# A convolution and a whitening on one core: pieces of the last pass hold one image, and the conv tiles x and y get two buffers each

## The chip, the cores and the metric

The kernel runs on one core of a Trainium2 chip. The metric is the time of one execution on the device in microseconds; the time before is a median of 928.11 us over 3 runs. The core has a matrix engine (PE, whose weight loads are listed apart as PEld), a vector engine (DVE), a scalar engine (ACT), GpSimd (POOL), and SP, which here does nothing but issue DMAs. Each engine works through its own list of instructions in order. All DMAs share the core's 16 DMA engines.

## The reference

Input x has 4 images of 64 channels of 256 x 256 pixels in float32. Two layers are computed:

- A convolution for each channel. Its kernel is the outer product of two filters of 256 taps, hx along one axis and hy along the other, that a small network with sines computes. So a channel's image is multiplied by one Toeplitz matrix on one side and by another on the other side: `y = conv(x, hx outer hy) + x * bias[channel]`.
- A whitening over the channels: with `x1` the result as a matrix of 64 rows (channels) and 262,144 columns (pixels of all images), `x1_s` every ninth column, `mean` its mean, `cov = x1_s @ x1_s.T / count + 0.01 I`, the output is `cov^(-1/2) @ (x1 - mean)`, with the inverse square root from five Newton-Schulz steps.

The whitening needs the covariance of all images before the first output can be computed, so the result of the convolution goes to memory (134 MB of traffic with the read back) and is read again in a last pass.

## The kernel before

**Stages.** First the filter network (to about 21 us of the span). Then the convolution (to 628 us). Then what is left of the covariance and the small matrix chain for the inverse square root (to 672 us). Then the last pass: pieces of y are read, multiplied by the whitening matrix, and written out (to 928 us).

**The convolution.** The work is cut in 32 steps `(g, n)`: eight channels (group g of 8) of image n. For g 0 to 5 the steps run over n within g; at the end they run over n, with g = 6 and 7 for each, so the last two groups of image 0 are done at steps 24 and 25, of image 1 at 26 and 27, and so on. A step is four channel pairs c = 0, 2, 4, 6, and one call of `group(first, second)` is made for each pair. It multiplies the pair `first` (its x tile) by the first Toeplitz matrix, and, interleaved on PE, the pair `second`, which had its first product two calls ago, by the second one (line 208). Then ACT copies the first product out of PSUM (line 338), and DVE computes `y = x * bias + product` for the second pair (line 343, two instructions). Up to three sampling copies on DVE follow (`pack`, line 252): they pick every ninth pixel of a finished y tile for the covariance, nine copies for each tile.

**The order on SP.** The lists of all engines are in program order (`tc.manual_schedule`). After the instructions of a group SP gets, in this order:

1. the store of the second pair to `y_d` (line 353), which waits for DVE's two y writes;
2. one load of a quarter of an x tile, two channels, 512 KB (line 103);
3. in some groups a part of a later filter matrix (line 178, 256 or 192 KB, 56 of them in all);
4. in some of the last groups one or two loads of pieces for the last pass (line 290, 2 MB each), as the table `early` says.

SP stands still while its next instruction waits for something. Which x quarter is loaded after which group is set by these lines:

```
part = (c - 2) // 2 % 4
to = i + 2 if c else i + 1
```

So the first quarter of step i+2 is sent after pair c = 2 of step i, the second after c = 4, the third after c = 6, and the fourth after c = 0 of step i+1: each is sent six groups before the group that first needs it. Tiles x ("in") and y ("out") come from one pool, `big`, with three buffers for each tag, 16 KB per partition a buffer.

**The last pass.** y is kept in two tensors `y_d[v]` of 128 rows, the 64 channels of image 2v and those of 2v+1. A piece `(v, q)` is 128 rows by 4096 pixels; there are 16 for each v. The pieces take over buffers of the convolution: `homes` lists 13 of them, `tssioitsoitos`, with t a filter matrix, s a sample tile, i an x tile, o a y tile; piece i goes to home i modulo 13. Eight pieces are sent before the convolution ends (`early`), five directly after, the others when a home has been written out. Each piece is multiplied by the whitening matrix for the upper and the lower 64 rows (line 521), shifted by ACT (line 526) and DVE (line 529), and written by a DMA that POOL issues (line 534). `covariance(n - 1)` (line 266) runs on PE before pair c = 4 of steps 27, 29 and 31.

## Time and profile before

| what | us |
|---|---|
| median of 3 runs (lowest, highest) | 928.11 (927.27, 928.23) |
| the profiled execution, its own time | 930.36 |
| its span | 928.2 |
| PE busy with matmuls in the span | 788.6 |
| DVE busy | 653.6 |
| ACT busy | 480.9 |
| filter stage / convolution / matrix chain / last pass, ends at | 21 / 628 / 672 / 928 |
| DMA, moved in the span | 285.56 MB, mean 308 GB/s |

The profile is of one execution. An engine's busy time counts its instructions, not its waits, and matmuls overlap, so a busy PE is not PE at its peak. A line "A <- B" among the waits says that A stood idle until B was done. For a DMA the time "to landing" runs from its issue on SP or POOL until its completion is signalled, so it holds the time that it stands behind other transfers. In the stretches, the last three numbers are the granted clock of PE (1.00 is full), the mean busy share of the DMA engines, and GB/s.

### The profile page before, as it was taken

Reading aid. Unit: us, or ns where it says so; the run is one execution under the profiler, and the core shown is the slowest. Engines: PE = TensorE matmul, PEld = TensorE weight load, DVE = VectorE, ACT = ScalarE, POOL = GpSimd, SP = SyncE. Lnnn points to the kernel's source line nnn. Section 1 sums busy time; section 2 is a strip of 40 time slices with the busy share of each in tenths; the row PEclk is TensorE's granted clock in tenths of the full one; section 3 lists DMA queues with packets and bytes.
Section 4 is the critical chain, followed back from the end, with each engine's and each line's share of the span. In section 5 each row is a group of like instructions: output and inputs, shape, how many; then the busy total and the mean of one; then the engine's idle time right before and its main releaser. Section 6 shows DMA issues by size and latency. Waiting matters only on the chain.

```text
span 928.2 us, 27807 instructions
## 1 busy us (share of the span) xinstructions
PE 788.6 (85%) x11814; PEld 631.0 (68%) x11814; DVE 653.6 (70%) x869; ACT 480.9 (52%) x791; POOL 31.8 (3%) x71
## 2 busy tenths in 40 slices
PE   3999999999999999999999999999787777765400
PEld 2899999999999999999999999998311111111100
DVE  3058687768777877787677866667599999996500
ACT  2345454545454544554554544441399888876500
POOL 3000000000000000000000000000010000000010
PEclk9999999999999999999999999999799999998755
DMA  4698888888888888879997769989999999999998
GB/s 145 189 275 257 251 258 261 248 258 258 252 251 262 260 248 261 262 237 280 284 277 236 234 189 332 326 288 392 417 407 429 430 428 429 431 430 431 431 430 340
DMA packets 115406, 285.56 MB, mean 308 GB/s; under 512 B 6831, under 2 KB 89172, under 8 KB 107604
## 3 DMA queue, kind: packets, MB, share of 16 engines
q1 hardware_dynamic: 108080, 216.08, 70.2%
q0 software_dynamic: 6336, 67.11, 17.0%
q8 instruction: 93, 1.52, 0.7%
q10 hardware_dynamic: 868, 0.60, 0.2%
q14 instruction: 29, 0.24, 0.1%
HBM read 149.35 MB, written 134.42 MB: 306 GB/s over the span
## 4 chain that ended last, share of the span: by engine, by line
PE 69%; issue 15%; DVE 9%; ACT 3%; DMA 2%; POOL 0%; POOLq 0%; ACTq 0%; DVEq 0%; SPq 0%
PE p L208 65%; DVE yi L529 8%; ACT yi L526 3%; DMA yi<-y_d 2%; PE pc L266 2%; PE pk L234 1%; POOL out_dram L534 0%; PE po L521 0%; DMA toep<-g_d 0%; DVE y L343 0%; PE ZY L436 0%; PE YT L436 0%; DVE scratch L154 0%; DVE samp L252 0%; PE pm L147 0%
## 5 line engine op out<-in xcount | busy, mean ns | idle before, releaser
L208 PE MATMUL p<-toep,x 64*64 64x64 f32 (+3 forms) x5120 | 595.6, 288 | 5.2 <-DMA toep<-g_d 4.7
L208 PE MATMUL p<-toep,o 64*64 64x64 f32 (+3 forms) x5120 | 589.2, 285 | 0.2
L208 PEld LDWEIGHTS p<-toep,x 64*128 64x128 f32 (+1 forms) x5120 | 548.3, 168 | 31.5 <-issue 5.6
L208 PEld LDWEIGHTS p<-toep,o 64*128 64x128 f32 (+1 forms) x5120 | 543.5, 166 | 11.8 <-POOLq L224 0.6
L338 ACT COPY o<-p 64x512 f32<-64x512 f32 x512 | 297.0, 580 | 317.9 <-PE p L208 310.1
L343 DVE SCALAR_TENSOR_TENSOR y<-x,bias,p 128x512 f32<-128x512 f32 x256 | 179.9, 743 | 162.7 <-PE p L208 162.2
L252 DVE COPY_PREDICATED samp<-mask,y 128x448 f32<-128x448 int32 (+3 forms) x288 | 281.0, 976 | 6.6
L529 DVE TENSOR_SCALAR yi<-po,shift 64x512 f32<-64x512 f32 x256 | 192.1, 750 | 23.4 <-PE po L521 16.7
L521 PE MATMUL po<-yi,W 64*64 64x512 f32 x1024 | 150.0, 653 | 63.1 <-DVE yi L529 40.9
L526 ACT ACTIVATE yi<-po,shift 64x512 f32<-64x512 f32 x256 | 174.9, 683 | 42.4 <-PE po L521 34.9
L521 PEld LDWEIGHTS po<-yi,W 64*64 64x64 f32 x1024 | 35.4, 141 | 176.9 <-DVE yi L529 127.8
L534 POOL DMA_DIRECT2D out_dram<-yi x44 | 23.7, 539 | 262.6 <-DVE yi L529 119.3
L420 POOL MEMSET chain<- 64x64 f32 x1 | 0.1, 146 | 616.6 <-PE p L208 616.6
L266 PEld LDWEIGHTS pc<-samp 128*64 128x64 f32 x464 | 14.4, 137 | 2.2 <-issue 1.4
L266 PE MATMUL pc<-samp 128*64 128x65 f32 x464 | 15.1, 223 | 0.7 <-ACT samp L243 0.4
L147 PE MATMUL pm<-scratch 128*128 128x128 f32 (+1 forms) x12 | 3.7, 466 | 8.8 <-ACT scratch L156 6.2
L274 DVE SCALAR_TENSOR_TENSOR cov<-pc,cov 128x65 f32<-128x65 f32 x4 | 0.9, 226 | 12.7 <-PE pc L266 12.7
L147 PEld LDWEIGHTS pm<-scratch 128*128 128x128 f32 (+1 forms) x12 | 2.9, 313 | 9.4 <-ACT scratch L156 6.8
L234 PE MATMUL pk<-y,pick 128*128 128x112 f32 (+1 forms) x36 | 7.7, 390 | 1.3 <-DVE y L343 1.3
L234 PEld LDWEIGHTS pk<-y,pick 128*128 128x128 f32 x36 | 7.3, 259 | 1.7 <-issue 1.7
L243 ACT COPY samp<-pk 128x116 f32<-128x116 f32 x1 | 0.3, 271 | 15.9 <-PE pk L234 15.9
L131 POOL TENSOR_SCALAR pick<-ident,rows 128x128 f32<-128x128 f32 x9 | 5.7, 649 | 0.0
(71 smaller groups left out, 41.8 us busy)
## 6 DMA issues: line engine op xcount, KB each, us to landing
x<-in_x_dram SPq DMA_DIRECT2D x128, 512.0 KB, 5.8
y_d<-y SPq DMA_DIRECT2D x128, 512.0 KB, 4.1
yi<-y_d SPq DMA_DIRECT2D x32, 2048.0 KB, 16.0
out_dram<-yi POOLq DMA_DIRECT2D x28, 2048.0 KB, 43.4
out_dram<-yi POOLq DMA_DIRECT2D x16, 512.0 KB, 8.4
toep<-g_d SPq DMA_DIRECT2D x28, 256.0 KB, 6.3
toep<-g_d SPq DMA_DIRECT2D x28, 192.0 KB, 5.7
toep<-g_d SPq DMA_DIRECT2D x2, 384.0 KB, 8.3
```

Source lines behind the costliest of these rows:

```text
L131: nc.gpsimd.tensor_scalar(pick[:, s, :], ident, rows[:, s : s + 1], None, ALU.mult)
L147: nc.tensor.matmul(pm, lhsT=wt, rhs=hs[u], start=True, stop=True)
L208: mm = nc.tensor.matmul(ps[q : q + w, m, HP * k : L], lhsT=src[parts, k // 2, m * P + q : m * P + q + w], rhs=t[parts, : stop : -1] if k e ...
L234: nc.tensor.matmul(pk[:, b, :, 0:nj], lhsT=pick[:, (s - b) % STEP, :], rhs=yt[:, cs, b, s : s + STEP * (nj - 1) + 1 : STEP], start=(s == 0 ...
L252: nc.vector.copy_predicated(dst, m, src)
L266: nc.tensor.matmul(pc[half], lhsT=samp[n][:, b, j, 0:C], rhs=samp[n][:, b, j, :], start=(b == 0 and j < 2), stop=(b == H2 - 1 and j >= NJ ...
L338: nc.scalar.copy(o1[to], units[u][0][0][fr])
L343: nc.vector.scalar_tensor_tensor(yt[:, c + u], xt[:, c + u], bias[:, ch : ch + 1], units[u][1][0], ALU.mult, ALU.add,)
L521: nc.tensor.matmul(po[u][halves[k]], lhsT=W[halves[u]], rhs=yt[halves[u], cols[k]], start=True, stop=True,)
L526: nc.scalar.activation(yt[halves[0], cols[k]], po[0][halves[k]], AF.Identity, bias=shift[halves[k]])
L529: nc.vector.tensor_scalar(yt[halves[1], cols[k]], po[1][halves[k]], shift[halves[k]], None, ALU.add)
L534: nc.gpsimd.dma_start(out=o[:, end - part : end], in_=yt[:, end - part : end])
```

## The change

It has these parts:

- `y_d` becomes four tensors, one for each image: 128 rows of 32,768 pixels, the upper half of the image's rows for 64 channels, then the lower half. A piece `(n, q)` holds one image; there are 8 for each n. The output tensor has the same layout, `(n, half, channel, pixel)`, and is put in the usual order on the host after the run.
- The store of a pair is issued as two DMAs, one for each half, 256 KB each.
- The pool `big` has two buffers for each tag in place of three; a new pool `epool` has two buffers of the same size, which only pieces use ("e"). The list of homes is `eetssitsoiots`, 13 as before.
- The x quarters: the first of step i+1 is sent after pair c = 4 of step i, the second after c = 6, the third after c = 0 of step i+1, the fourth after c = 2.
- The table `early` has other places: eight loads as before, the first after pair c = 4 of step 26 (before: step 28).

```diff
-    big = ctx.enter_context(tc.tile_pool(name="big", bufs=3))
+    big = ctx.enter_context(tc.tile_pool(name="big", bufs=2))
+    epool = ctx.enter_context(tc.tile_pool(name="epool", bufs=2))
...
-    y_d = [dram.tile([2 * C, PIX], F32, tag=f"y{v}", name=f"y_d{v}") for v in range(NB // 2)]
+    y_d = [dram.tile([H2 * C, PIX // H2], F32, tag=f"y{n}", name=f"y_d{n}") for n in range(NB)]
...
-    pieces = [(v, q) for v in range(NB // 2) for q in range(PIX // FP)]
+    pieces = [(n, q) for n in range(NB) for q in range(PIX // H2 // FP)]
...
-        {"t": (tpool, "toep"), "s": (spool, "samp"), "i": (big, "in"), "o": (big, "out")}[k]
-        for k in "tssioitsoitos"
+        {"t": (tpool, "toep"), "s": (spool, "samp"), "i": (big, "in"), "o": (big, "out"), "e": (epool, "extra")}[k]
+        for k in "eetssitsoiots"
...
-        nc.sync.dma_start(out=t, in_=y_d[v][:, q * FP : (q + 1) * FP])
+        nc.sync.dma_start(out=t, in_=y_d[n][:, q * FP : (q + 1) * FP])
...
-    early = {(28, 4): 1, (28, 6): 1, (29, 6): 1, (30, 4): 1, (31, 2): 1, (31, 4): 1, (31, 6): 2}
+    early = {(26, 4): 1, (26, 6): 1, (27, 4): 1, (28, 2): 1, (29, 6): 1, (31, 4): 2, (31, 6): 1}
...
-            row = n % 2 * C + g * CG + c
-            nc.sync.dma_start(
-                out=y_d[n // 2][row : row + 2, :].rearrange(
-                    "c (b p w) -> p (c b) w", p=P, w=L
-                ),
-                in_=yt[:, c : c + 2].rearrange("p c b w -> p (c b) w"),
-            )
+            for b in range(H2):
+                row = b * C + g * CG + c
+                nc.sync.dma_start(
+                    out=y_d[n][row : row + 2, :].rearrange("c (p w) -> p c w", w=L),
+                    in_=yt[:, c : c + 2, b],
+                )
...
-            xt = loaded_x.pop((g, n))
+            xt = loaded_x[g, n]
...
-                part = (c - 2) // 2 % 4
-                to = i + 2 if c else i + 1
-                if to < len(steps) and to > 1:
+                part = (c - 4) // 2 % 4
+                to = i + 1 if c >= 4 else i
+                if 1 < to < len(steps):
...
-        o = out[2 * v : 2 * v + 2].rearrange("u c h w -> (u c) (h w)")[:, q * FP : (q + 1) * FP]
+        o = out[n].rearrange("b c f -> (b c) f")[:, q * FP : (q + 1) * FP]
...
-    out = nc.dram_tensor("out_0_dram", (NB, C, L, L), F32, kind="ExternalOutput").ap()
+    out = nc.dram_tensor("out_0_dram", (NB, H2, C, PIX // H2), F32, kind="ExternalOutput").ap()
...
-    return r.results[0]["out_0_dram"]
+
+    y = np.asarray(r.results[0]["out_0_dram"]).reshape(NB, H2, C, PIX // H2)
+    return np.ascontiguousarray(y.transpose(0, 2, 1, 3)).reshape(NB, C, L, L)
```

More of the change, by code (lines that the diff above doesn't have):

```diff
@@ L274, in covariance @@
         nc.vector.scalar_tensor_tensor(cov, pc, 1.0 / NSAMP, cov, ALU.mult, ALU.add)
-    pieces = [(v, q) for v in range(NB // 2) for q in range(PIX // FP)]
+    pieces = [(n, q) for n in range(NB) for q in range(PIX // H2 // FP)]
     homes = [
-        {"t": (tpool, "toep"), "s": (spool, "samp"), "i": (big, "in"), "o": (big, "out")}[k]
-        for k in "tssioitsoitos"
+        {"t": (tpool, "toep"), "s": (spool, "samp"), "i": (big, "in"), "o": (big, "out"), "e": (epool, "extra")}[k]
+        for k in "eetssitsoiots"
     ]
     def load_y(i):
-        v, q = pieces[i]
+        n, q = pieces[i]
         pool, tag = homes[i % len(homes)]
-        t = pool.tile([P, FP], F32, tag=tag, name=f"yi_{v}_{q}")
-        nc.sync.dma_start(out=t, in_=y_d[v][:, q * FP : (q + 1) * FP])
+        t = pool.tile([P, FP], F32, tag=tag, name=f"yi_{n}_{q}")
+        nc.sync.dma_start(out=t, in_=y_d[n][:, q * FP : (q + 1) * FP])
         return t
@@ L506, in conv_whiten_kernel @@
     halves = [slice(u * C, (u + 1) * C) for u in range(2)]
-    for i, (v, q) in enumerate(pieces):
+    for i, (n, q) in enumerate(pieces):
         yt = loaded.pop(i)
-        o = out[2 * v : 2 * v + 2].rearrange("u c h w -> (u c) (h w)")[:, q * FP : (q + 1) * FP]
+        o = out[n].rearrange("b c f -> (b c) f")[:, q * FP : (q + 1) * FP]
         part = FP if 1 < i < len(pieces) - 2 else FP // 4
@@ L515, in conv_whiten_kernel @@
             po = [
-                psA.tile([P, 512], F32, tag="psA", name=f"po_{v}_{q}_{w}_{u}") for u in range(2)
+                psA.tile([P, 512], F32, tag="psA", name=f"po_{n}_{q}_{w}_{u}") for u in range(2)
             ]
```

## The prediction

> **What bounds the kernel now.** I read the stages first (busy time of each engine in stretches of the span, with granted clock, share of the DMA engines and GB/s):

> ```profile
> 60.00:628.40 568.40, 567.65 (x10063) 533.64 (x10062) 427.87 (x519) 281.47 (x486) 0.00 (x0) 1.00 0.85 262
> 628.40:672.00 43.60, 34.83 (x325) 25.31 (x323) 26.02 (x58) 10.22 (x21) 1.95 (x4) 0.80 1.01 410
> 672.00:928.20 256.20, 141.89 (x968) 32.84 (x967) 186.34 (x249) 169.28 (x248) 21.91 (x41) 0.87 0.99 419
> ```

> The first pair after the length is PE, the second its weight loads. Up to 628.4 PE has no gap (567.65 of 568.40 us): the convolution is bound by matmuls. From 628.4 on the DMA engines are full (1.01 and 0.99): the tail of 300 us is bound by bytes. So a change is worth something in the first stage only through PE, and in the tail only through bytes that were moved before 628.4.

> Next, whether PE ever waited for an x tile. Of all waits of line 208's matmuls on a DMA there is one, on a filter matrix at the start:

> ```profile
> PE p L208 <- DMA toep<-g_d: 4.7, 1, 4.7
> ```

> Then the pace of a group, from the timelines of SP and of DVE (start, length, instruction):

> ```profile
> 309.86 0.38 SPq L353 DMA_DIRECT2D y_d<-y  x1
> 310.28 0.50 SPq L103 DMA_DIRECT2D x<-in_x_dram  x1
> 310.82 1.48 SPq L178 DMA_DIRECT2D toep<-g_d  x1
> 314.08 0.38 SPq L353 DMA_DIRECT2D y_d<-y  x1
> 314.55 0.45 SPq L103 DMA_DIRECT2D x<-in_x_dram  x1
> ```
> ```profile
> 308.42 1.40 DVE L343 SCALAR_TENSOR_TENSOR y<-x,bias,p 128x512 f32<-128x512 f32 x2 [0.50 <-PE p L208]
> 309.75 2.99 DVE L252 COPY_PREDICATED samp<-mask,y 128x448 f32<-128x448 int32 x3
> 312.65 1.40 DVE L343 SCALAR_TENSOR_TENSOR y<-x,bias,p 128x512 f32<-128x512 f32 x2
> 317.56 1.41 DVE L343 SCALAR_TENSOR_TENSOR y<-x,bias,p 128x512 f32<-128x512 f32 x2 [3.52 <-PE p L208]
> ```

> Two groups take 317.56 - 308.42 = 9.14 us, one g = 4.57 us. PE releases DVE at 308.42, when it is about to begin the next group; DVE writes y until 309.82; SP, which was standing in that wait, sends the store at 309.86, 1.44 us after the group's end, and only then the x load behind it in its order. How long the x load takes, from issue to landing, least, median and most: over the whole kernel, then between 323 and 333 us, where no filter load stands in between:

> ```profile
> x<-in_x_dram SPq DMA_DIRECT2D x128, 512.0 KB, 5.8
> y_d<-y SPq DMA_DIRECT2D x128, 512.0 KB, 4.1
> ```
> ```profile
> DMA to landing us min/median/max: 4.6/4.8/5.0
> ```

> Today this latency costs nothing, since an x load is sent six groups (27 us) before its use.

> **The change part by part.**

> *x in two buffers: the lead shrinks from six groups to one.* The load of channels c, c+1 is now sent after group k, and group k+2 needs it in its very first matmuls; only group k+1 lies between. Only SP's order counts, and there the load still stands behind the store of group k. So, from the end of group k: 1.44 us to the store; from the store's issue to the landing of x 0.42 + 4.8 = 5.22 us; about 0.3 us (estimate, one weight load of 0.17 us and one matmul of 0.29 us from their rows, partly overlapped) until matmuls flow again. That is D = 6.96 us, and the cover is g = 4.57 us. End(k+2) = End(k) + D + g, hence 11.53 us for two groups where 9.14 were: 5.77 a group, +1.20. Steps 2 to 31 have 120 such groups: **+144 us**. Queued behind the waiting matmul on PE is the whole group, the second-stage products of the previous group too; ACT's copies, DVE's two y writes and SP's next store wait for that, and behind the store the next x load: the delay feeds itself, so it does not dissolve. Bounds: x landing at its overall median of 5.8 gives D = 7.96, 6.27 a group, +203; the shortest chain (the 314.08 store, 1.1 us after its group's end by the cadence, x at its least 4.4 us, a restart of 0.1 us) gives D = 6.0, 5.3 a group, +86. I take the value near +144, because the slower pace drains the queues: the DMA share of 0.85 becomes 0.85 x 4.57 / 5.77 = 0.67, as in the quiet stretch.

> [...]

> *Each store in two halves.* 128 DMAs of 512 KB become 256 of 256 KB. SP spends 0.42 us more per group. This puts the x load 0.42 us later, but its data start only when the store's 512 KB are through, more than 0.42 us after either way, so I cost it at nothing; uncovered it is 0.42 / 2 x 120 = +25 us. The packets stay 1 KB.

> *y in two buffers.* Step i first writes y in its third group; y of step i-2 is stored for good three groups earlier (landing 4.1 us) and its nine sampling copies, three a group, end two groups earlier. Nothing, unless DVE falls two groups (9 us) behind: it has 1.40 + 2.99 = 4.4 us of work a group.

> *Piece loads at step 26 instead of 28.* Eight of 2 MB still precede the end of the convolution, five of them now ahead of x loads that have no slack. In the old kernel those between 560 and 632 us took

> ```profile
> DMA to landing us min/median/max: 9.4/11.3/16.1
> ```

> and y stores behind them up to 14.7. At 430 GB/s 2 MB occupy the engines for 4.9 us. After x has landed, some 7 us after its group's end, the piece runs to 12; the next group's store, sent at 5.8 + 1.4 = 7.2 us, would have begun its data near 8, and starts near 12: 3 to 4 us late, and so its x load. Five loads at 3.3: **+16 us** (0 if they fall into gaps, 25 if all their bytes count). The covariance of an image, 116 matmuls before steps 27 and 29, 3.7 us, now runs while PE would wait: **-4**.

> *The tail.* At the end of the convolution as many pieces are loaded as before (five landed, three on their way), 13 slots are filled before the first result leaves, and reads and writes keep runs of 16 KB. One piece is sent 4.3 us earlier: **-2**, at best one piece, -5. Whether the other addresses change the 430 GB/s I can't see; 1% of 256 us is 2.6 either way.

> The sum on the profiled execution's span of 928.2 us: 144 + 16 - 4 - 2 = +154, 1082 us. That execution took 930.36 us in all, the median of the runs is 928.11; the same difference on the median gives **1082 us**.

> *The clock.* [...] The rows (stretches as above, clock third from the end):

> ```profile
> 648.00:660.00 12.00, 6.49 (x90) 4.87 (x85) 4.05 (x22) 2.28 (x7) 0.00 (x0) 0.74 1.01 424
> 720.00:780.00 60.00, 42.98 (x312) 8.79 (x312) 58.17 (x79) 53.11 (x78) 5.35 (x10) 1.00 1.01 430
> ```

> PE busy for 54% had 0.74, busy for 72% in short pieces 1.00. After the change PE is busy for 4.57 / 5.77 = 79%, with gaps of 1.2 us, or 2.4 us every second group. [...] if gaps at the piece loads did halve it, their few groups would cost some +5 more; if it fell throughout, see below.

> **Rivals.**
> 1. *The queue stays congested:* landing keeps the 5.8 us of the crowded stretches, since the load starts sooner after its store, and filter loads (56 of 256 or 192 KB) follow it. For it: the median itself; against it: the smaller DMA share. +203 + 16 - 6 = +213, 1140 us.
> 2. *The load is faster than I think*[...], 1015 to 1025 us.
> 3. *The clock falls:* matmuls at 0.75 would make g 6.1 us, (6.96 + 6.1) / 2 = 6.5 a group, +235, some 1170 us; at half clock more. Against it the 72% row.
> 4. *The other side:* PE doesn't wait, and the tail gains its piece: 923 to 928 us. This needs x to land within 4.57 us of the end of group k. It decides from D = g: the load would have to be on its way about 2.4 us earlier, which it can't while it stands behind a store that waits for DVE (1.44 us alone leaves 3.1 us, under the least landing of 4.4). That the change doesn't do what it says is the same case: the buffers do shrink and the order is written by hand.

> **How the numbers follow.** Chances: my case 0.56 (1050 to 1115), rival 1 0.21, rival 2 0.13, rival 3 0.06, rival 4 0.04. The likeliest is 1082 us. For 8 in 10 the range takes in most of rivals 1 and 2: 1022 to 1150. A difference under 0.2% can't be told from none here; faster 0.025, same 0.015, slower 0.96.

> **What would show it.** Right: matmuls of line 208 wait for x loads (none now), some 120 x 1.2 = 144 us in about 60 to 120 waits; PE's share of the convolution falls near 80%; the DMA share there falls below 0.75; the two y writes follow each other at 11.5 us per two groups; the landing of x near 5; the tail after the last product still 300 us. Wrong: x landing above 6 (rival 1), below 4.4 (rival 2), a clock under 0.95 before 630 us (rival 3), or PE without gaps (rival 4). The forecast falls most easily through the landing of x: each 0.1 us is 6 us of the total.

## The result: 1181.4 us in place of 928.2, all of it in the convolution

The changed kernel takes 1181.37 us (median of 4 runs, 1172.58 to 1186.53), the kernel before 928.17 us on the same chip; the ratio is 1.272 with an interval of 1.262 to 1.281. The forecast was 1082 us, in a range of 1022 to 1150: the direction was right, the loss was 253 us where 154 had been worked out. The times and ratios below leave out executions over 1.5% above the fastest of their kernel: one of four of the changed kernel without early pieces, and two of four with one filler matmul, the profiled one of 1136.76 us among them.

The profiled execution of the changed kernel took 1172.58 us, its span is 1170.8. Split at the last of DVE's y writes, the stretches of the kernel before (PE busy follows the length; granted clock, DMA share and GB/s stand at the end) are

```profile
60.00:636.60 576.60, 575.75 (x10142) 540.58 (x10140) 435.86 (x529) 283.09 (x488) 0.15 (x1) 1.00 0.85 263
636.60:928.20 291.60, 168.62 (x1212) 51.21 (x1210) 204.37 (x296) 177.88 (x265) 23.71 (x44) 0.86 0.99 419
```

and of the changed kernel

```profile
60.00:879.10 819.10, 663.62 (x10102) 618.18 (x10092) 437.12 (x530) 282.83 (x488) 0.14 (x1) 0.91 0.60 188
879.10:1170.80 291.70, 169.79 (x1211) 52.00 (x1210) 204.21 (x296) 177.87 (x265) 23.63 (x44) 0.84 0.99 418
```

The tail is the same to 0.1 us. The convolution is 242.5 us longer, and the row says how. PE stands idle for 819.1 - 663.6 = 155.5 us, where it was 0.9. It is also *busy* for 87.9 us more, with the same matmuls. The granted clock explains most of that. Its records in the trace have 143 us at half clock in this stretch, and PE was busy in 134 of them; half of that, some 67 us, is lost. (The mean of 0.91 would give 72 us, but it counts half clock while PE stands idle too.) About 21 us are left; 61 waits with a restart of 0.3 us each would make about that much, but no run separates it.

Among the waits of the changed kernel, the new row stands fourth:

```profile
PE p L209 <- DMA x<-in_x_dram: 147.3, 67, 4.6
```

67 waits for x loads, 2.2 us each on the mean, 4.6 at the most, so one for about every second group of the 120. The loads themselves are not slow; they land sooner than before, in 4.9 us from issue where it was 5.8, while the DMA share fell from 0.85 to 0.60:

```profile
x<-in_x_dram SPq DMA_DIRECT2D x128, 512.0 KB, 4.9
y_d<-y SPq DMA_DIRECT2D x256, 256.0 KB, 2.8
```

The pace is read from the y writes in the timeline of DVE:

```profile
322.97 1.41 DVE L344 SCALAR_TENSOR_TENSOR y<-x,bias,p 128x512 f32<-128x512 f32 x2 [5.95 <-PE p L209]
327.28 1.40 DVE L344 SCALAR_TENSOR_TENSOR y<-x,bias,p 128x512 f32<-128x512 f32 x2
337.03 1.41 DVE L344 SCALAR_TENSOR_TENSOR y<-x,bias,p 128x512 f32<-128x512 f32 x2 [5.46 <-PE p L209]
341.23 1.41 DVE L344 SCALAR_TENSOR_TENSOR y<-x,bias,p 128x512 f32<-128x512 f32 x2
350.33 1.41 DVE L344 SCALAR_TENSOR_TENSOR y<-x,bias,p 128x512 f32<-128x512 f32 x2 [7.69 <-PE p L209]
354.64 1.40 DVE L344 SCALAR_TENSOR_TENSOR y<-x,bias,p 128x512 f32<-128x512 f32 x2
```

Two groups take 350.33 - 322.97 = 27.36, halved 13.7 us, where 11.53 had been forecast and 9.14 is needed. They come in a pair 4.3 us apart, then there is a gap. What happens in the gaps is seen in stretches of 3.41 us of the same time (PE busy after the length, clock third from the end):

```profile
303.85:307.27 3.42, 1.62 (x17) 1.41 (x15) 3.35 (x5) 1.80 (x4) 0.00 (x0) 1.00 0.69 239
307.27:310.68 3.41, 3.41 (x73) 3.29 (x69) 0.75 (x2) 0.00 (x0) 0.00 (x0) 1.00 0.96 251
...
327.75:331.16 3.41, 0.61 (x7) 0.57 (x7) 3.34 (x5) 1.65 (x3) 0.00 (x0) 1.00 0.81 272
331.16:334.57 3.41, 3.41 (x21) 3.41 (x19) 0.41 (x1) 0.00 (x0) 0.00 (x0) 0.50 0.50 165
```
```profile
341.40:344.81 3.41, 1.29 (x12) 0.91 (x11) 1.24 (x2) 1.96 (x4) 0.00 (x0) 1.00 0.75 245
344.81:348.23 3.42, 3.42 (x23) 3.42 (x21) 0.00 (x0) 0.00 (x0) 0.00 (x0) 0.50 0.59 183
```

After a stretch with 1.80 us of idle time (the first row) the clock stays at 1.00; after 2.80 us and after 2.12 us of it the clock is 0.50 for the next 3.41 us. (The counts of matmuls in these rows are not to be compared, since their shapes differ.) What half clock costs is read from the groups that start after a wait: from the first matmul to DVE's y write they take 4.72 us at full clock and 6.41 us where a half-clock stretch falls into them (medians of 26 and 34), 1.7 us more, which is half of 3.41.

### The profile page after: what moved, and what is told of

It is laid out like the page before. It is cut to its first block, busy times and chain, and to the rows that moved or that the text cites. A ratio compares the mean times of both kernels' runs of the same rounds, so it can differ in the third digit from the quotient of the medians.

```text
span 1170.8 us, 27960 instructions
## 1 busy us (share of the span) xinstructions
PE 877.5 (75%) x11814; PEld 709.4 (61%) x11814; DVE 655.0 (56%) x869; ACT 480.8 (41%) x791; POOL 31.7 (3%) x71
## 4 chain that ended last, share of the span: by engine, by line
PE 40%; DMA 25%; DVE 18%; issue 13%; SPq 3%; ACT 0%; POOL 0%; POOLq 0%; DVEq 0%; ACTq 0%
PE p L209 36%; DMA x<-in_x_dram 24%; DVE yi L529 9%; DVE y L344 6%; SPq L355 3%; DVE samp L253 2%; PE pc L267 1%; PE pk L235 1%; PE po L521 0%; DMA y_d<-y 0%; POOL out_dram L534 0%; DMA toep<-g_d 0%; PE ZY L436 0%; DVE scratch L155 0%; PE YT L436 0%
## 5 line engine op out<-in xcount | busy, mean ns | idle before, releaser
L209 PE MATMUL p<-toep,x 64*64 64x64 f32 (+3 forms) x5120 | 680.5, 304 | 160.3 <-DMA x<-in_x_dram 147.3
L209 PEld LDWEIGHTS p<-toep,x 64*128 64x128 f32 (+1 forms) x5120 | 590.3, 178 | 198.6 <-issue 73.1
L209 PE MATMUL p<-toep,o 64*64 64x64 f32 (+3 forms) x5120 | 670.1, 302 | 0.1
L209 PEld LDWEIGHTS p<-toep,o 64*128 64x128 f32 (+1 forms) x5120 | 589.3, 176 | 10.0 <-POOLq L225 0.6
L529 DVE TENSOR_SCALAR yi<-po,shift 64x512 f32<-64x512 f32 x256 | 192.0, 750 | 24.7 <-PE po L521 18.5
L534 POOL DMA_DIRECT2D out_dram<-yi x44 | 23.6, 537 | 262.8 <-DMA out_dram<-yi 109.4
## 6 DMA issues: line engine op xcount, KB each, us to landing
x<-in_x_dram SPq DMA_DIRECT2D x128, 512.0 KB, 4.9
out_dram<-yi POOLq DMA_DIRECT2D x16, 512.0 KB, 9.4
```

The source lines that it names most:

```text
L209: mm = nc.tensor.matmul(ps[q : q + w, m, HP * k : L], lhsT=src[parts, k // 2, m * P + q : m * P + q + w], rhs=t[parts, : stop : -1] if k e ...
L529: nc.vector.tensor_scalar(yt[halves[1], cols[k]], po[1][halves[k]], shift[halves[k]], None, ALU.add)
L534: nc.gpsimd.dma_start(out=o[:, end - part : end], in_=yt[:, end - part : end])
```

## The experiments

My first theory after the result: the short lead of the x loads is the whole cause; it makes gaps of some 155 us, the gaps set off the half clock, which I then put at 72 us, and restarts cost the rest. The rivals: halved stores, buffers or the pieces cost something themselves; or the matmuls are slow for another reason than the clock.

**The order of the x loads alone, in the kernel before.**

```diff
-            xt = loaded_x.pop((g, n))
+            xt = loaded_x[g, n]
...
-                part = (c - 2) // 2 % 4
-                to = i + 2 if c else i + 1
-                if to < len(steps) and to > 1:
+                part = (c - 4) // 2 % 4
+                to = i + 1 if c >= 4 else i
+                if 1 < to < len(steps):
```

> The kernel before with one difference: x quarters are sent where the change sends them, with three buffers of x and y, whole stores, the old pieces. Theory: nearly the whole loss appears, 1140 to 1190 us, PE waits of 130 to 160 us for x, and half clock in the convolution. Rival (the buffers or the halved stores make the loss): under 1000 us.

1176.05 us, ratio 1.264 (1.261 to 1.268). With three buffers, whole stores and the old pieces the loss is there in full:

```profile
60.00:889.00 829.00, 673.83 (x10142) 628.27 (x10140) 436.39 (x529) 282.87 (x488) 0.14 (x1) 0.90 0.60 185
```

PE idle 155.2 us, clock 0.90. Of the idle time the trace puts 127.6 us down to x loads in so many words; 26.4 us more are booked on DVE's sampling copies, but those 11 matmuls too start 0.1 us after their x load has landed (for the ten whose landing is recorded). So it is where the loads stand in SP's order, not the buffers as such.

**Two groups of lead in place of one, still with two buffers.** The changed kernel with

```diff
-                part = (c - 4) // 2 % 4
-                to = i + 1 if c >= 4 else i
+                part = (c - 2) // 2 % 4
+                to = i + 1 if c >= 2 else i
```

> The changed kernel with one difference: each x quarter is sent one group earlier (two groups of lead in place of one), still with two x buffers. Theory (the loss is the short lead alone): End(k+3) = End(k) + D + g gives (6.96 + 4.57) / 3 = 3.84 us a group, under g = 4.57, so PE has no waits for x, the clock stays at 1.00 before 630 us, and the time is 924 to 934 us. Rival (halved stores, two y buffers or the earlier piece loads cost much themselves): above 950 us, with waits of PE that do not come from x loads.

938.94 us, ratio 1.011 (1.009 to 1.013): 243 of the 253 us are gone, with one more group of lead. It missed its range by 5 us, and is far from the rival's.

```profile
60.00:646.20 586.20, 579.46 (x10148) 543.37 (x10144) 436.88 (x530) 283.10 (x488) 0.14 (x1) 1.00 0.84 263
```

The convolution ends 9.6 us later than before the change, with 6.7 us of idle time and one stretch at half clock. Step by step it takes 18.3 to 18.5 us nearly everywhere, as before the change, and loses most in steps 27, 28 and 30, at 2 MB pieces. To test that:

**The same without early pieces.**

```diff
-    early = {(26, 4): 1, (26, 6): 1, (27, 4): 1, (28, 2): 1, (29, 6): 1, (31, 4): 2, (31, 6): 1}
+    early = {(31, 4): 6, (31, 6): 2}
```

> Two groups of lead for x as in the run with that lead, and none of the eight early pieces before step 31 (six after its pair 4, two after pair 6). Theory (the 10 us that two groups of lead still lose come from 2 MB pieces ahead of x loads): the convolution ends at 628 to 630 us as before the change, and the last pass pays for the bytes, some 10 to 20 us, so the time is 936 to 950. Rival (two groups are too few anyway): the convolution still ends 8 us or more later than before the change.

952.41 us, ratio 1.026 (1.025 to 1.028), slightly above the range. (Its 628 us are the last product of an x tile, which ends at 628.4 before the change and at 627.5 here; the rows are split at the last y write.)

```profile
60.00:635.70 575.70, 574.87 (x10140) 539.83 (x10136) 435.94 (x529) 283.62 (x488) 0.14 (x1) 1.00 0.81 249
635.70:950.50 314.80, 184.45 (x1212) 61.98 (x1210) 204.31 (x296) 178.38 (x265) 23.71 (x44) 0.79 0.99 421
```

The convolution ends at 635.7, as before the change (636.6). So two groups of lead suffice, and what they still lost was the pieces ahead of x loads. The tail became 314.8 - 291.2 = 23.6 us longer than in the run before it (937.4 - 646.2 = 291.2): that is what five pieces loaded early are worth, 4.7 us each, about the time of 2 MB at the 421 GB/s of this row (5.0 us).

**The changed kernel without early pieces** (the same line in it).

> The changed kernel with none of the eight early pieces before step 31. The forecast's step (five pieces ahead of x loads cost 16 us of the convolution): it ends 12 to 20 us earlier than in the changed kernel (at 851 to 859 in place of 870). Rival (the steps with pieces take no longer than the others in the trace, so they cost nothing): it ends within 5 us of 870, and the whole is 10 to 25 us slower through the tail.

1187.5 us, ratio 1.272 (1.265 to 1.279). Up to step 26 this is the same program as the changed kernel. From the first y write of step 26 on, the changed kernel and then this one have

```profile
725.80:879.10 153.30, 130.02 (x2122) 120.74 (x2112) 84.36 (x105) 51.04 (x88) 0.14 (x1) 0.92 0.68 234
730.40:874.80 144.40, 128.69 (x2124) 119.59 (x2112) 83.86 (x104) 51.13 (x88) 0.15 (x1) 0.93 0.54 176
874.80:1188.80 314.00, 178.64 (x1212) 59.60 (x1210) 204.27 (x296) 178.39 (x265) 23.71 (x44) 0.81 1.00 422
```

The stretch with the pieces is 8.9 us shorter without them, 7.6 us of it idle time of PE. Over the whole convolution only 4.3 us are left of this, since up to step 26 the changed kernel happened to be 4.6 us faster, with the same instructions. So the pieces cost some 9 us, good to about 5. The last product of an x tile ends at 866.6 in place of 870.9 us, which is inside the rival's 5 us, but only through those 4.6 us of chance; neither the forecast's 16 us nor the rival's nothing is shown. The tail is 22.3 us longer; the whole is 6 us slower on the medians, while executions of one kernel differ by 14 us and more.

**Three x buffers and six groups of lead, everything else of the change kept** but for one of the two slots and one entry of `early` (a piece after pair 4 of step 30, none after pair 4 of step 27).

```diff
+    xpool = ctx.enter_context(tc.tile_pool(name="xpool", bufs=3))
-    epool = ctx.enter_context(tc.tile_pool(name="epool", bufs=2))
+    epool = ctx.enter_context(tc.tile_pool(name="epool", bufs=1))
...
-        return big.tile([P, CG, H2, L], F32, tag="in", name=f"x_{g}_{n}")
+        return xpool.tile([P, CG, H2, L], F32, tag="in", name=f"x_{g}_{n}")
...
-        {"t": (tpool, "toep"), "s": (spool, "samp"), "i": (big, "in"), "o": (big, "out"), "e": (epool, "extra")}[k]
-        for k in "eetssitsoiots"
+        {"t": (tpool, "toep"), "s": (spool, "samp"), "i": (xpool, "in"), "o": (big, "out"), "e": (epool, "extra")}[k]
+        for k in "etssiitsoiots"
...
-    early = {(26, 4): 1, (26, 6): 1, (27, 4): 1, (28, 2): 1, (29, 6): 1, (31, 4): 2, (31, 6): 1}
+    early = {(26, 4): 1, (26, 6): 1, (28, 2): 1, (29, 6): 1, (30, 4): 1, (31, 4): 2, (31, 6): 1}
...
-                part = (c - 4) // 2 % 4
-                to = i + 1 if c >= 4 else i
-                if 1 < to < len(steps):
+                part = (c - 2) // 2 % 4
+                to = i + 2 if c else i + 1
+                if to < len(steps) and to > 1:
```

> The changed kernel with three x buffers again and each x quarter sent six groups ahead, as before; y keeps two buffers, one slot is kept for pieces (homes etssiitsoiots, of eight early pieces the fifth after pair 4 of step 30); image-wise pieces and halved stores stay. Theory (only the short lead costs): no waits for x, full clock up to the end of the convolution, 923 to 931 us. Rival (halved stores, two y buffers or image-wise pieces cost or gain by themselves): outside 915 to 940.

928.72 us, ratio 1.0002 (0.9992 to 1.0012): no difference, and inside the range.

```profile
60.00:635.40 575.40, 575.13 (x10132) 539.65 (x10122) 435.97 (x530) 283.61 (x488) 0.14 (x1) 1.00 0.84 264
635.40:926.10 290.70, 170.53 (x1211) 51.93 (x1210) 204.27 (x296) 178.42 (x265) 23.71 (x44) 0.84 1.00 419
```

So halved stores, two y buffers and pieces of one image cost nothing together while the x loads have six groups of lead. They bring nothing either: 13 slots are filled in both kernels, the DMA engines are full through the tail (share 0.99 before the change, 1.00 here, at 419 GB/s both times), and the bytes are the same.

**Filling the gaps with useless matmuls.** To separate the clock from the waiting, PE gets work that the wait covers, two matmuls here, and one or three in two other kernels:

```diff
+        if first is not None and first[0] * NB + first[1] > 1:
+            for _ in range(2):
+                nc.tensor.matmul(
+                    units[0][0][0][:, 0, :], lhsT=ident, rhs=second[5][0][:, 0, :],
+                    start=True, stop=True, skip_group_check=True,
+                )
         toeplitz_products(units, orders[0])
```

> The changed kernel with two additional matmuls of 128x256 before each group from step 2 on ([...] into a bank that the group then starts afresh)[...]. Theory (stall of about 155 us, and on top of it half clock that the gaps set off, about 72 us, and some 15 us of restarts): gaps shrink from 2.2 us to under 1.6, the clock stays at 1.00 and the time falls to 1095 to 1115 us although work was added. Rival (the matmuls are slow for another reason, such as contention for SBUF or a full queue): 1180 us or more.

> The same with three such matmuls[...]. Theory: no gaps worth the name, full clock[...], 1085 to 1110 us. Rival: 1190 us or more.

> The changed kernel with one additional matmul of 128x256 before each group[...]. Theory (PE goes to half clock for 3.41 us after a stretch of 3.41 us in which it stood idle for more than about 1.9 us): the longest gaps shrink from 2.4 to about 2.0 us, half clock falls from 143 us to between 20 and 80, and the time to 1120 to 1155 us. Rival (any gap lowers the clock in proportion): half clock 115 us or more and 1165 us or more.

One matmul: 1125.8 us, ratio 1.213 (1.205 to 1.221). Two: 1126.39 us, 1.212 (1.209 to 1.214). Three: 1146.45 us, 1.234 (1.232 to 1.236). The stretches, one, two and three:

```profile
60.00:843.70 783.70, 701.84 (x10334) 599.01 (x10324) 445.68 (x529) 283.16 (x488) 0.14 (x1) 0.97 0.64 197
```
```profile
60.00:833.00 773.00, 736.23 (x10624) 631.04 (x10620) 446.30 (x529) 282.86 (x488) 0.14 (x1) 0.99 0.65 200
```
```profile
60.00:851.60 791.60, 777.48 (x10822) 668.14 (x10812) 446.94 (x529) 282.63 (x488) 0.14 (x1) 1.00 0.65 195
```

All three are faster than the changed kernel although each does more work, and the clock goes from 0.91 to 0.97, 0.99 and 1.00. One matmul is inside its range. Two missed theirs by 11 us and three by 36. A filler costs more than I had allowed for without a measurement: the trace has two instructions for each of the 360 fillers with three a group, and together they keep PE busy for 187.5 us, 0.52 us each:

```profile
L334 PE MATMUL p<-o,ident 128*128 128x256 f32 x720 | 187.5, 396 | 0.0
L334 PEld LDWEIGHTS p<-o,ident 128*128 128x128 f32 x720 | 126.9, 189 | 35.6 <-issue 18.9
```

With three, PE is busy for 777.5 of 791.6 us, so the fillers themselves set the pace. Without their 187.5 us it is busy for 590 us: nearly the 575.8 us of the kernel before, where the changed kernel has 663.6 for the same matmuls. The rival, under which the clock is not the cause, asked for 1180 us and more; it falls. What these runs don't give is a sharp border for the fall of the clock: with one filler two falls follow a stretch with only 1.65 and 1.69 us of idle time, while one with 1.81 us is followed by full clock. Idle time of PE alone does not tell it exactly.

## Why the prediction was wrong in size

*"The lead shrinks from six groups to one ... +144 us"*: right in place, somewhat too small in size. PE waits for x loads where none was, in pairs of groups, and the order alone, put into the old kernel, gives the whole loss. The chain that the forecast drew stands in the trace; here it is from the y write at 350.33 above, with the two halves of the store, the x load, its landing and the first matmul after it:

```profile
351.77 0.87 SPq L355 DMA_DIRECT2D y_d<-y  x2
352.74 0.44 SPq L104 DMA_DIRECT2D x<-in_x_dram  x1
```
```profile
352.74 4.78 DMA x<-in_x_dram
357.52 0.14 issue
357.65 4.42 PE p L209 x24
```

Over the 61 waits of more than 0.8 us the medians are: 1.43 us from the y write to the store, 0.97 to the x load, 4.9 to its landing, 0.14 to the first matmul. The whole, D, is 7.57 us where 6.96 had been worked out. From the store to the landing it is some 5.9 us where 5.22 was taken: the row of 4.8 us for the landing fits when counted from the load's own issue, but this now comes 0.97 us after the store, not 0.42. The halves are not the reason, since the old kernel with the new order has 0.42 and then 5.3, nearly the same in all. By itself 0.6 us in 60 pairs is some 37 us.

*"PE busy for 54% had 0.74, busy for 72% in short pieces 1.00"*: **this is the step that failed.** From it the forecast put the clock at nothing, and the clock took some 67 us. I had compared averages: 72% busy in the last pass at full clock, 79% expected here. But the 28% in the last pass, between 720 and 780 us, are gaps of at most 0.46 us, and those here are 2.3 us in one piece (median; mean 2.5). In the trace of the changed kernel the falls go with the idle time inside one stretch of the grid of 3.41 us, 1.84 us or more before each of the 34, and not with the mean, which was 81% busy (663.6 of 819.1 us).

The trace of the kernel before could have shown it. The forecast's own row from 648 to 660 us, with the clock at 0.74, holds this pair of stretches:

```profile
650.28:653.70 3.42, 0.57 (x4) 0.38 (x4) 1.66 (x10) 1.84 (x4) 0.00 (x0) 1.00 1.00 422
653.70:657.11 3.41, 2.06 (x10) 1.35 (x10) 1.29 (x9) 0.21 (x1) 0.00 (x0) 0.50 1.03 442
```

The longest gap there begins at 651.79 and lasts 2.35 us, about what the forecast expected for every second group, and half clock follows. Between 720 and 780 us, where the clock is 1.00, no stretch of the grid has more than 1.24 us idle. (Idle time does not tell it exactly here either: right after the convolution a single gap, 1.35 us before the change and 1.34 us after it, is followed by half clock.)

The sign "a clock under 0.95 before 630 us" had been named, and came: 0.91. The rival with a falling clock got 6% and 1170 us, nearest to what came, but in part by luck: with the clock at 0.75 it has some 52 us of waiting and 183 us of slower matmuls, where 155 and 88 were measured.

*The restart.* It stood with 0.3 us in D, 18 us in all. From landing to the first matmul it is 0.14 us; some 21 us of longer busy time that the clock does not explain may be the rest of it.

*"Each store in two halves ... nothing"*: right. The run with six groups of lead has slack enough to hide a cost, so the better witness is the old kernel with the new order: its D is 7.64 us, with whole stores, against 7.57. *"y in two buffers: nothing"*: right, by the runs with three x buffers and with two groups of lead.

*Piece loads, +16, and the covariance, -4*: the pieces cost some 9 us, with an uncertainty of about 5; with two groups of lead, 10. The covariance's 4 us (it runs before pair c = 4 of steps 27, 29 and 31) no run separates.

*The tail, -2*: 291.7 against 291.6 us, nothing.

The sum: for the convolution the forecast had 144 + 16 - 4 = 156 us, and 242.5 came. Of the difference of 86 us, 67 are the clock; the other 20 belong to a D that was taken too short, less what the pieces did not cost. Two slips of the working changed nothing: rival 2's 1015 to 1025 us, an estimate of mine, leave out the +10 of the other terms, and what is called a group's end is DVE's first y write, 0.55 us before PE is through (median), at both ends of the sum.

## What to carry to other kernels

A load's lead is counted on the queue that issues it: from the moment at which the instruction ahead of it is released, not from where the buffer comes free. Here one group of lead, 4.57 us, against 7.6 us from one group's y write to the first matmul that its x load allows, cost a quarter of the run with what the clock added; one more group of lead, with the same two buffers, took nearly all of it back. And when a wait is put on PE, cost it twice: the wait, and the half-speed stretch of 3.41 us that followed here, at 1.7 us of lost work each, where PE had been idle for 1.84 us or more of the stretch before. On an average busy share this can't be seen; on stretches of 3.41 us it can, in the trace of the kernel before too.

## What the runs showed of the hardware that I had not expected

The clock's records in the convolution of the changed kernel are of two kinds only, 1.00 and 0.50, and the commonest cycle is 3.41 us at half and 10.24 us at full clock, together 13.65 us. Two groups there take 13.3 us on the mean, and where the falls follow each other 14.06, 13.30 and 13.73. So the kernel's cycle and the clock's are nearly the same length; whether one holds the other, no run tests.

Useless work made the kernel faster: 240 fillers, 136 us of PE's busy time, took 55 us off the changed kernel.
